# A four-layer graph network: edge payloads scattered by source inside layer 0, and one-hot matrices stored there for layer 2

## The chip, the cores and the metric

The kernel runs on one core of one Trainium2 chip. The metric is the device time of one execution in microseconds (us). It has 25,000 edges and 50,000 nodes of 64 values each.

## The reference

Four layers follow each other, each added to its input `x` after `h = relu(layernorm(x))`. All use the same edges, sorted by target (`dst`).

```python
# layer 0: messages from both ends, mean over the target's edges, update
messages = relu(concat([h[src], h[dst]]) @ W_msg + b_msg)
aggregated = segment_sum(messages, dst) / max(count(dst), 1)
x = x + relu(concat([h, aggregated]) @ W_upd + b_upd)
# layer 1: normalised sum over the edges, product
x = x + (segment_sum(h[src] * norm, dst) + h) @ W.T + b
# layer 2: attention over each target's edges (4 heads), edge-type tables,
#          two layer norms around a gelu network
x = x + layer_norm(x1 + gelu(x1 @ W1 + b1) @ W2 + b2) * g + b   # x1: after attention
# layer 3: exp(-t*L) applied to h by Taylor series over the edges, by SOURCE:
term = scale * segment_sum(edge_weight * term[dst], src) / k    # 4 x 20 terms
```

Layer 3 sums by source, while layers 0 to 2 sum by target. A Taylor term of order k is not zero only at a node from which a path of k edges leads on.

## The kernel before

**Tiling.** The function `fast` holds the work. Nodes lie in 392 blocks of 128 (`BK`); 49 groups (`NQ`) of eight blocks are the steps `q` of every layer. Each group owns 640 edge slots, five tiles of 128. So a step gathers 5 tiles of source rows with indirect DMAs on GpSimd (POOL), 128 rows each, brings edges to nodes and nodes to edges with 0/1 matrices on TensorE (PE), and stores its nodes' rows to tables in HBM.

**0/1 matrices.** `node_hot` makes `noh` (8 instructions on VectorE, DVE; from slot to node), `slot_hot` makes `soh` (5 instructions; from node to slot), by comparing keys with an iota. Layer 0 needs both, layer 1 `soh`, layer 2 both: `noh` in `hots`, `soh` in the second `message`. The keys come from `ktab`, broadcast to 128 partitions (`load_keys`).

**Preparation** (lines 1210 to 1489). Histograms of the edges (196 tiles), each edge's slot by source (`slot`, `pf`), and then the payload: `raw` holds 16 words for each edge, source, target's row, weight, and a mark whether the target has edges of its own. The mark comes from 196 gathers (`gather(raw[:, t, 3:4], otab, ...)`), and 196 scatters send the payload to its slot in the table `stab` (`scatter(stab, raw[:, t, :], pf[:, t:t + 1], ...)`). `layer0_tables` makes the norms and products of layer 0's nodes (`atab`, `btab`, `h0t`), 49 steps on DVE, ACT and PE. Between its steps the hook `region` reads each half group's edges from `fields` with a DMA on SP at an offset that a register holds (`rl`, 98 of them). From `rl` follow keys, counts (`kf`, `cnt`, `ci`, `di`), the gather rows `nrs`, and the degrees (`deg`, 49 one-hots).

**Lists for layer 3.** `build_lists` is a generator: it reads `stab` back, then `list_two` compacts the slots that have a second term (one-hots on DVE, products on PE), `flags_two` and `looks` ask with 98 gathers (`lgot`) whether the path goes on, then `list_three`, and `compact` for orders 4 to 8, each with `link`, `map_rows` and `looks` (scatters and gathers on POOL). A `Pace` runs it beside the layers: after each stage of a step it adds `rate` to its credit and takes one piece of the generator for each whole credit. The rates are 0.5 in layer 0, 0.4 in layer 1, 1.2 in layer 2. A `yield "wait"` sets the credit back.

**Layers.** `pipeline` runs the stages of a layer skewed over the steps: layer 0 has `fetch, hots, message, sums, update, project`, layer 1 `fetch, scaled, sums, turn, product`. Layer 2 has two pipelines, `up` (`fetch, hots, logits`) and `down` (`fetch2, message, sums, attend, turn, close, product, finish`), in four batches with a softmax after each batch; `down` is one batch behind. Layer 3 applies terms 1 and 2 to all nodes, and terms 3 to 8 to the lists, with `dense` for the rest.

**Order.** Each engine runs its instructions in the order that the program's scheduler wrote when the kernel was built. That order is not quite the order of the calls: an instruction is placed early when its engine is expected to be free. What it writes holds at run time. POOL runs one queue: an indirect DMA that waits holds back all behind it.

Of the kernel before, what the change touches and what calls it, by code (L numbers as in the profile page):

```python
# [55 lines left out]
BW = 3 * D  # L56
# [4 lines left out]
OHW = (0, 384, 768, 1152, 1664, 1920)  # L61

# [904 lines left out]
def fast(ctx: ExitStack, tc: tile.TileContext, a: dict, out: bass.AP, flag: bass.AP):  # L967
# [187 lines left out]
    def layer0_tables(hook):  # L1155
        with tc.tile_pool(name="pac", bufs=1) as cp, tc.tile_pool(name="pa", bufs=3) as pool, \
# [25 lines left out]
            def product(q, s):  # L1182
# [10 lines left out]
                pack(b3, bt.rearrange("p b (k d) -> p b k d", k=3))  # L1193
# [24 lines left out]
    with tc.tile_pool(name="so", bufs=1) as sp, tc.tile_pool(name="sw", bufs=4) as sw:  # L1218
# [14 lines left out]
        fld = sp.tile([P, NT, 3], I32, name="fld")  # L1233
        for i, t in enumerate((dstt, srct, typt)):
            nc.vector.tensor_copy(fld[:, :, i], t)
        nc.sync.dma_start(fields[0:EP, :].rearrange("(p t) f -> p (t f)", p=P), fld.rearrange("p t f -> p (t f)"))
# [6 lines left out]
        tail = sp.tile([P, RW * 3 // P], I32, name="tail")  # L1243
# [53 lines left out]
        nc.sync.dma_start(otab.rearrange("(p b) o -> p (b o)", p=P), hasout)  # L1297


        nrd = sp.tile([P, NT], I32, name="nrd")  # L1300
        raw = sp.tile([P, NT, PW], I32, name="raw")
        lo, hi = sp.tile([P, NT], I32, name="lo"), sp.tile([P, NT], I32, name="hi")
        nc.vector.tensor_scalar(hi, dstt, N - 1, None, op0=OP.min)
        nc.vector.tensor_scalar(lo, hi, P - 1, None, op0=OP.bitwise_and)
        nc.vector.tensor_scalar(hi, hi, 7, None, op0=OP.arith_shift_right)
        nc.vector.scalar_tensor_tensor(nrd, lo, float(BK), hi, op0=OP.mult, op1=OP.add)
# [88 lines left out]
        for t in range(NT):  # L1395
            put = scatter(stab, raw[:, t, :], pf[:, t:t + 1], P * TL - 1)
            if t:
                tc.declare_no_dep(put.ins, group="slots", reason="rows are distinct")
            tc.add_to_no_dep_group("slots", put.ins)


        rl = sp.tile([NQ, RW, 3], I32, name="rl")
# [50 lines left out]
        srci = sp.tile([P, NQ, 5], I32, name="srci")  # L1453
        with tc.tile_pool(name="ps3", bufs=3, space=PSUM) as ps:
            for row, dst in ((kf, key), (srow, srci), (ci, cinv), (di, dise)):
# [16 lines left out]
        nc.vector.tensor_copy(khi, hi)  # L1472
        deg = sp.tile([P, BK], F32, name="deg")
# [216 lines left out]
    def list_two(cols):  # L1690
# [3 lines left out]
        nc.vector.tensor_copy(live, cols[3])  # L1694
# [155 lines left out]
    def build_lists():  # L1850

        for _ in range(6):
            yield "wait"
# [27 lines left out]
    def node_hot(pool, s):  # L1881

        s.noh = pool.tile([P, 8, 2 * P], BF16, name="noh")
        for j in range(8):
            t0, n = BT[j]
            nc.vector.tensor_scalar(s.noh[:, j, :n * P], s.keys[:, t0 * P:(t0 + n) * P], pblk[:, j:j + 1], None,  # L1886
# [11 lines left out]
    def to_slots(po, s, tab, start=True):  # L1898

        for i in range(5):  # L1900
            b0, nb = TB[i]
            for j in range(b0, b0 + nb):
                c = (i - BT[j][0]) * P
                for k in range(3):
                    nc.tensor.matmul(po[:, i, :], s.noh[:, j, c:c + P], tab[:, j, k * D:k * D + D],
                                     start=(start and j == b0 and k == 0), stop=(j == b0 + nb - 1 and k == 2))
# [753 lines left out]
```

## Time and profile before

| | us |
|---|---|
| median of 13 runs | 3649.52 (3629.94 to 3668.43) |
| profiled execution, its time | 3648.63 |
| profiled execution, its span | 3646.5 |
| busy: PE, DVE, ACT, POOL | 2524.8, 2660.1, 1325.0, 2095.3 |
| mean granted TensorE clock | 0.678 |
| DMA, mean rate | 126 GB/s |

The profile is of one execution. Instruction lines give the line of the source, engine, operation, output and input by the program's names, shapes, count, then the busy time in us and the mean of one in ns, then the idle time of the engine before them and what ended most of it. "issue" is time in which the engine waited for nothing that the profile shows. A wait is attributed to the release that came last. Line numbers are those of the kernel before; the changed kernel's are higher by 2 to 16.

### The profile page before, as it was taken

Reading aid. Unit: us, or ns where it says so; the run is one execution under the profiler, and the core shown is the slowest. Engines: PE = TensorE matmul, PEld = TensorE weight load, DVE = VectorE, ACT = ScalarE, POOL = GpSimd, SP = SyncE. Lnnn points to the kernel's source line nnn. Section 1 sums busy time; section 2 is a strip of 40 time slices with the busy share of each in tenths; the row PEclk is TensorE's granted clock in tenths of the full one; section 3 lists DMA queues with packets and bytes.
Section 4 is the critical chain, followed back from the end, with each engine's and each line's share of the span. In section 5 each row is a group of like instructions: output and inputs, shape, how many; then the busy total and the mean of one; then the engine's idle time right before and its main releaser. Section 6 shows DMA issues by size and latency. Waiting matters only on the chain. (4 is left out here: it accounts for less than half of the span.)

```text
span 3646.5 us, 63671 instructions
## 1 busy us (share of the span) xinstructions
PE 2524.8 (69%) x21828; PEld 1782.3 (49%) x21828; DVE 2660.1 (73%) x8365; ACT 1325.0 (36%) x3056; POOL 2095.3 (57%) x1997
## 2 busy tenths in 40 slices
PE   7897775689999746777579667677687464456620
PEld 3324664577777634666455334344343354355520
DVE  9999988788788637999878767778888565455310
ACT  0002552222222315777405443445478333332000
POOL 0477777733334757666376775664100677674786
PEclk9755555776566857888758676778789675566555
DMA  1003772754445416787664333333222345488221
GB/s 53 6 4 108 209 228 93 188 144 123 111 126 138 121 32 182 234 241 233 183 192 141 89 106 107 99 116 99 71 89 74 117 118 155 147 234 227 44 25 11
DMA packets 528804, 457.79 MB, mean 126 GB/s; under 512 B 282147, under 2 KB 388802, under 8 KB 528340
## 3 DMA queue, kind: packets, MB, share of 16 engines
q1 hardware_dynamic: 361204, 263.52, 25.5%
q10 hardware_dynamic: 94032, 139.60, 11.1%
q0 software_dynamic: 73232, 50.49, 7.5%
q8 instruction: 174, 2.85, 0.3%
q14 instruction: 162, 1.33, 0.1%
HBM read 217.09 MB, written 237.38 MB: 125 GB/s over the span
## 5 line engine op out<-in xcount | busy, mean ns | idle before, releaser
L1006 POOL DMA_INDIRECT y<-h3tab,sptr x245 | 262.4, 1071 | 326.4 <-DVE soh L1894 252.0
L1006 POOL DMA_INDIRECT ga<-atab,nrs x245 | 248.2, 1013 | 313.2 <-DVE z L2003 144.2
L1006 POOL DMA_INDIRECT kvg<-kvtab,nrs x245 | 249.1, 1017 | 178.7 <-issue 65.5
L1006 POOL DMA_INDIRECT gt<-g1tab,nrs x245 | 254.5, 1039 | 145.6 <-issue 65.8
L1934 PEld LDWEIGHTS <-soh 128*128 128x128 bf16 x4410 | 224.1, 118 | 206.0 <-issue 192.9
L1924 PE MATMUL pa<-soh,m 128*64 128x256 bf16 (+1 forms) x2646 | 282.0, 331 | 35.8 <-ACT m L2006 24.4
L1006 POOL DMA_INDIRECT raw<-otab,nrd x196 | 194.9, 994 | 192.0 <-DVE bad L1152 132.6
L1011 POOL DMA_INDIRECT stab<-raw,pf x196 | 207.2, 1057 | 59.7 <-issue 59.4
L1924 PEld LDWEIGHTS <-m 128*64 128x64 bf16 x2646 | 178.2, 140 | 119.1 <-issue 51.0
L1934 PE MATMUL po<-y,soh 128*128 128x64 bf16 x2205 | 126.0, 232 | 133.8 <-DVE y L1086 67.4
L1006 POOL DMA_INDIRECT lgot<-nmap,ldst x183 | 183.9, 1005 | 59.8 <-issue 53.3
L1131 DVE TENSOR_REDUCE ln_v<-ln_sq 128x8 f32<-128x512 f32 x294 | 196.0, 678 | 24.8 <-ACT ln_sq L1144 18.7
L1894 DVE TENSOR_SCALAR soh<-it,key 128x384 bf16<-128x384 f16 (+2 forms) x735 | 204.7, 320 | 6.0 <-PE pa L1924 5.7
L1006 POOL DMA_INDIRECT y<-ftab,ldst x140 | 139.5, 997 | 85.4 <-issue 74.7
L1144 ACT ACTIVATE ln_sq<-ln_xc 128x512 f32<-128x512 f32 x196 | 121.0, 627 | 172.9 <-DVE ln_xc L1142 168.3
L1086 DVE TENSOR_TENSOR y<-y 128x320 f32<-128x320 f32 (+1 forms) x196 | 76.0, 391 | 146.3 <-ACT y L2493 123.0
L1886 DVE TENSOR_SCALAR noh<-keys,pblk 128x256 bf16<-128x256 f16 (+1 forms) x784 | 177.8, 288 | 2.7 <-DMA keys<-ktab 2.7
L1189 PE MATMUL pab<-wab,tr 64*128 64x128 f32 x784 | 149.8, 436 | 32.4 <-ACT tr L1176 32.4
L1132 ACT ACTIVATE ln_v<-ln_v,epsc 128x8 f32<-128x8 f32 x294 | 83.5, 296 | 228.3 <-DVE ln_v L1131 208.2
L1934 PE MATMUL po<-g,soh 128*128 128x64 bf16 x2205 | 119.6, 213 | 67.0 <-DVE g L1086 66.6
L2352 PE MATMUL ph<-tr,w1z 128*128 128x512 f32 x196 | 144.0, 825 | 27.4 <-ACT tr L2346 27.1
L1189 PEld LDWEIGHTS pab<-wab,tr 64*128 64x128 f32 x784 | 135.8, 324 | 51.4 <-ACT tr L1176 51.1
(571 smaller groups left out, 7399.3 us busy)
## 6 DMA issues: line engine op xcount, KB each, us to landing
kvtab<-kv SPq DMA_DIRECT2D x49, 512.0 KB
xs<-xstab SPq DMA_DIRECT2D x98, 256.0 KB
ftab<-f ACTq DMA_DIRECT2D x98, 256.0 KB
xt<-in_x SPq DMA_DIRECT2D x96, 256.0 KB
btab<-bt ACTq DMA_DIRECT2D x49, 384.0 KB
bt<-btab SPq DMA_DIRECT2D x49, 384.0 KB
qtab<-qt ACTq DMA_DIRECT2D x49, 384.0 KB
qt<-qtab SPq DMA_DIRECT2D x49, 384.0 KB
```

The lines of the kernel that those rows point to most:

```text
L1006: return nc.gpsimd.indirect_dma_start(out=dst, out_offset=None, in_=tab[:, :], in_offset=IndirectOffsetOnAxis(ap=idx, axis=0))
L1011: return nc.gpsimd.indirect_dma_start(out=tab[:, :], out_offset=IndirectOffsetOnAxis(ap=idx, axis=0), in_=src, in_offset=None, bounds_chec ...
L1086: nc.vector.tensor_sub(x3[:, :, k, :], x3[:, :, k - 1, :], h[:, :, k - 1, :])
L1131: nc.vector.tensor_reduce(v, sq, AX.X, OP.add)
L1132: nc.scalar.activation(v, v, AF.Sqrt, bias=epsc, scale=1.0 / D)
L1144: nc.scalar.activation(sq, xc, AF.Square)
L1189: nc.tensor.matmul(pab[:, i, :], s.tr[r, i, :], wab[r, :], start=True, stop=True)
L1886: nc.vector.tensor_scalar(s.noh[:, j, :n * P], s.keys[:, t0 * P:(t0 + n) * P], pblk[:, j:j + 1], None, op0=OP.is_equal)
L1894: nc.vector.tensor_scalar(oh[:, OHW[i]:OHW[i + 1]], it16[:, b0 * P:(b0 + n) * P], keys[:, q, i:i + 1], None, op0=OP.is_equal)
L1924: nc.tensor.matmul(o, l, r, start=first, stop=last)
L1934: nc.tensor.matmul(po[:, j, :], oh[:, c:c + P], msg[:, i, k, :], start=(not started and i == t0 and k == 0), stop=(end and (not started or ...
L2352: nc.tensor.matmul(ph, w1z[h], s.tr, start=True, stop=True)
```

## The change

The diff, cut to its core:

```diff
-BW = 3 * D
+BW = 3 * D + 2
+NOH = (0, 128, 384, 640, 896, 1152, 1408, 1664)
-    fields = dram.tile([EPD, 3], I32, name="fields")
+    fields = dram.tile([EPD, 5], I32, name="fields")
+    paytab = dram.tile([P * NQ, 5 * PW], I32, name="paytab")
-    otab = dram.tile([NN, 1], I32, name="otab")
+    ohtab = dram.tile([NQ * P, 2, OHW[-1]], BF16, name="ohtab")
...
 # layer0_tables.product
+                nc.vector.tensor_copy(bt[:, :, 0:2], hasout[:, 8 * q:8 * q + 8, None].to_broadcast([P, 8, 2]))
...
 # preparation
-        nc.sync.dma_start(otab..., hasout)
-        nc.vector.memset(raw, 0)
-        for i, f in enumerate((srct, nrd, wt.bitcast(I32))):
-            nc.vector.tensor_copy(raw[:, :, i], f)
-        for t in range(NT):
-            gather(raw[:, t, 3:4], otab, nrd[:, t:t + 1])
...
-        for t in range(NT):
-            put = scatter(stab, raw[:, t, :], pf[:, t:t + 1], P * TL - 1)
+        fld = sp.tile([P, NT, 5], I32, name="fld")          # was written first, with 3 fields
+        for i, t in enumerate((dstt, srct, typt, wt.bitcast(I32), pf)):
+            nc.vector.tensor_copy(fld[:, :, i], t)
+        nc.scalar.dma_start(fields[0:EP, :]..., fld...)
-        rl = sp.tile([NQ, RW, 3], I32, name="rl")
+        rl = sp.tile([NQ, RW, 5], I32, name="rl")
...
+        nc.vector.memset(pay, 0)                            # weight, slot, row, source by group
+        nc.scalar.dma_start(paytab..., pay...)
...
 # build_lists
-        for _ in range(6):
-            yield "wait"
+        yield "wait"
...
 # layer 0
+            nc.sync.dma_start(s.pay..., paytab...[:, q, :])          # fetch
+            nc.sync.dma_start(ohtab[P * q:P * q + P, 0, :], s.noh)   # message
+            nc.scalar.dma_start(ohtab[P * q:P * q + P, 1, :], s.soh)
-            pe = ps.tile([P, 5, D], F32, name="pe", bufs=2)
+            pe = ps.tile([P, 5, D + 2], F32, name="pe", bufs=2)
+            nc.scalar.activation(s.pay.bitcast(F32)[:, :, 3], pe[:, :, 0], AF.Copy)
+            for i in range(5):                                       # sums
+                put = scatter(stab, s.pay[:, i, :], s.pay[:, i, 4:5], P * TL - 1)
-        lists_pace.rate = 0.5
-        pipeline(range(NQ), (fetch, hots, message, sums, update, project), lists_pace)
+        pipeline(range(NQ), (fetch, hots, message, sums, update, project))
 # layer 1
-            nc.scalar.dma_start(nodes(x2tab, q), x2)
+            nc.vector.tensor_add(x2b, x2, along(b2n, 8))
+            nc.scalar.dma_start(nodes(x2tab, q), x2b)
-        lists_pace.rate = 0.4
+        lists_pace.rate = 0.8
 # layer 2
-            load_keys(pool, q, s)
+            nc.sync.dma_start(s.noh, ohtab[P * q:P * q + P, 0, :])   # fetch
-            node_hot(pool, s)                                        # hots
+            nc.sync.dma_start(s.soh, ohtab[P * q:P * q + P, 1, :])   # fetch2
-            s.soh = slot_hot(pool, key, q)                           # message
-            nc.vector.tensor_add(s.x2, s.x2, along(b2n, 8))          # finish
-            nc.vector.tensor_add(x3, x3, h)
 # layer 3
+            nc.sync.dma_start(s.h, nodes(h3tab, q))                  # fetch
+            nc.vector.tensor_add(s.xs, s.xs, s.h)                    # scaled
```

The 196 gathers of the mark and the 196 scatters by edge order go. The slot `pf` and the weight travel as two more fields to the groups; each layer 0 step scatters its five tiles, 245 in all. The mark of the target is two more columns of `btab`, and comes out of the product with `noh` in `message`. Layer 0 runs no list work; layer 1 runs it at rate 0.8. `noh` is packed to 1920 columns, and it and `soh` are stored by layer 0 to `ohtab` (480 KB each a step) and loaded by layer 2. The add of `b2n` goes from layer 2 to layer 1, and the add of `h` to layer 3.

More of the change, by code (lines that the diff above doesn't have):

```diff
@@ L1453, in fast @@
         srci = sp.tile([P, NQ, 5], I32, name="srci")
+        wrow, prow = sp.tile([NQ, RW], F32, name="wrow"), sp.tile([NQ, RW], F32, name="prow")
+        nc.vector.tensor_copy(wrow, rl[:, :, 3].bitcast(F32))
+        nc.vector.tensor_copy(prow, rl[:, :, 4])
+        nc.vector.scalar_tensor_tensor(prow, prow, -float(FAR), own, op0=OP.add, op1=OP.mult)
+        nc.vector.tensor_scalar_add(prow, prow, float(FAR))
+        pay = sp.tile([P, NQ, 5, PW], I32, name="pay")
+        nc.vector.memset(pay, 0)
         with tc.tile_pool(name="ps3", bufs=3, space=PSUM) as ps:
-            for row, dst in ((kf, key), (srow, srci), (ci, cinv), (di, dise)):
+            for row, dst in ((kf, key), (srow, srci), (ci, cinv), (di, dise), (wrow, pay[:, :, :, 2].bitcast(F32)),
+                             (prow, pay[:, :, :, 4])):
                 pt = ps.tile([P, 5, NQ], F32, name="pt")
@@ L1472, in fast @@
         nc.vector.tensor_copy(khi, hi)
+        nrow = sp.tile([P, NQ, 5], F32, name="nrow")
+        nc.vector.scalar_tensor_tensor(nrow, lo, float(BK), hi, op0=OP.mult, op1=OP.add)
+        nc.vector.scalar_tensor_tensor(pay[:, :, :, 1], rowi[:, :NQ, None].to_broadcast([P, NQ, 5]), 8.0, nrow,
+                                       op0=OP.mult, op1=OP.add)
+        nc.vector.tensor_copy(pay[:, :, :, 0], srci)
+        nc.scalar.dma_start(paytab.rearrange("(p q) f -> p (q f)", p=P), pay.rearrange("p q i f -> p (q i f)"))
         deg = sp.tile([P, BK], F32, name="deg")
@@ L1881, in node_hot @@
     def node_hot(pool, s):
-        s.noh = pool.tile([P, 8, 2 * P], BF16, name="noh")
+        s.noh = pool.tile([P, OHW[-1]], BF16, name="noh")
         for j in range(8):
             t0, n = BT[j]
-            nc.vector.tensor_scalar(s.noh[:, j, :n * P], s.keys[:, t0 * P:(t0 + n) * P], pblk[:, j:j + 1], None,
+            nc.vector.tensor_scalar(s.noh[:, NOH[j]:NOH[j] + n * P], s.keys[:, t0 * P:(t0 + n) * P], pblk[:, j:j + 1], None,
                                     op0=OP.is_equal)
@@ L1896, in slot_hot, with to_slots @@
         return oh
[L1898 removed]
+    def to_slots(po, s, tab):
         for i in range(5):
@@ L1993, in fetch @@
             load_keys(pool, q, s)
+            s.pay = pool.tile([P, 5, PW], I32, name="pay", bufs=4)
+            nc.sync.dma_start(s.pay.rearrange("p i f -> p (i f)"), paytab.rearrange("(p q) f -> p q f", p=P)[:, q, :])
         def hots(q, s):
@@ L2009, in sums @@
         def sums(q, s):
+            for i in range(5):
+                put = scatter(stab, s.pay[:, i, :], s.pay[:, i, 4:5], P * TL - 1)
+                if q or i:
+                    tc.declare_no_dep(put.ins, group="slots", reason="rows are distinct")
+                tc.add_to_no_dep_group("slots", put.ins)
             pa = ps.tile([P, 512], F32, name="pa")
@@ L2305, in fetch2 @@
             nc.sync.dma_start(s.vv.rearrange("p t d -> p (t d)"), vvtab[P * q:P * q + P, :])
+            s.soh = pool.tile([P, OHW[-1]], BF16, name="soh", bufs=3)
+            nc.sync.dma_start(s.soh, ohtab[P * q:P * q + P, 1, :])
             s.h2 = pool.tile([P, 8, D], F32, name="h2", bufs=3)
```

41 lines of the change are left out of this document (16 added, 25 removed).

## The prediction

> **What bounds the kernel now.** I read the stage view first (busy time of each engine between two times). The cuts are the first gathers of the layers, which the views by tile give: `ga` at 658.4, `gt` at 1372.6, `kvg` at 1789.3, `y<-h3tab` at 2845.4 us. The columns are stretch, length, then busy time of PE, PEld, DVE, ACT, POOL, then granted clock, DMA share, GB/s. The first four rows are preparation, layer 0, layer 1, layer 2.
>
> ```profile
> 0.00:658.00 658.00, 490.99 (x2235) 285.24 (x2235) 602.04 (x1996) 161.27 (x353) 403.39 (x398) 0.61 0.34 97
> 658.00:1372.00 714.00, 605.56 (x5901) 486.67 (x5902) 519.29 (x1836) 191.86 (x492) 343.13 (x343) 0.66 0.47 126
> 1372.00:1789.00 417.00, 301.00 (x3533) 238.11 (x3533) 371.14 (x1096) 290.20 (x882) 254.53 (x245) 0.84 0.74 221
> 1789.00:2845.00 1056.00, 747.91 (x5474) 440.34 (x5475) 828.63 (x2542) 498.10 (x825) 518.76 (x498) 0.74 0.36 108
> ```
>
> DVE bounds the preparation (602 of 658) and layer 1 (371 of 417). The 398 POOL instructions of the preparation lie beside DVE. Layer 0 and layer 2 are not one thing each, so I cut them finer: plain layer 0, layer 0 with the list work of `list_two` in it, layer 0 with the `lgot` gathers in it, and the middle of layer 2.
>
> ```profile
> 671.00:745.00 74.00, 66.95 (x816) 54.70 (x817) 62.30 (x212) 28.50 (x74) 50.19 (x51) 0.85 0.92 237
> 873.00:1040.00 167.00, 164.42 (x1374) 132.06 (x1373) 122.54 (x451) 41.45 (x108) 56.28 (x54) 0.50 0.41 114
> 1223.00:1329.00 106.00, 55.04 (x555) 44.40 (x553) 43.27 (x136) 19.63 (x50) 80.41 (x85) 0.64 0.19 54
> 2000.00:2590.00 590.00, 415.86 (x2947) 242.48 (x2946) 453.05 (x1474) 264.96 (x449) 364.84 (x346) 0.74 0.34 101
> ```
>
> By the starts of `z` a step of layer 0 takes 8.2 to 9 us plain, 16.2 us in the second row (PE full, at half clock) and 19 to 22 us in the third (POOL full). In the fourth row 346 POOL instructions stand; with 0.30 us before each they fill 365 + 104 = 469 of 590 us, and the rest is mostly POOL waiting for list values from DVE. So POOL paces the middle of layer 2.
>
> The costliest groups give the prices: count, busy us and mean ns of one, idle before it.
>
> ```profile
> L1006 POOL DMA_INDIRECT ga<-atab,nrs x245 | 248.2, 1013 | 313.2 <-DVE z L2003 144.2
> L1006 POOL DMA_INDIRECT gt<-g1tab,nrs x245 | 254.5, 1039 | 145.6 <-issue 65.8
> L1011 POOL DMA_INDIRECT stab<-raw,pf x196 | 207.2, 1057 | 59.7 <-issue 59.4
> L1894 DVE TENSOR_SCALAR soh<-it,key 128x384 bf16<-128x384 f16 (+2 forms) x735 | 204.7, 320 | 6.0 <-PE pa L1924 5.7
> L1886 DVE TENSOR_SCALAR noh<-keys,pblk 128x256 bf16<-128x256 f16 (+1 forms) x784 | 177.8, 288 | 2.7 <-DMA keys<-ktab 2.7
> ```
>
> The waits around 650 us show all that the end of the preparation owes to the scatters:
>
> ```profile
> DVE bupd_o L1104 <- DMA stab<-raw,pf: 9.4, 1, 9.4
> POOL ga L1006 <- DVE bupd_o L1109: 2.6, 1, 2.6
> ```
>
> **The change part by part**, against the profiled execution (span 3646.5, time 3648.6; the median is 3649.5). A difference below 0.3%, 11 us, cannot be told from none.
>
> **Preparation.** 196 gathers of `otab` and 196 scatters leave POOL, but they were beside DVE: only the 9.4 + 2.6 us come back. DVE gains 49 copies of `hasout` into `bt` (0.21 us, as the 128x8 rows `ln_s` have: 10 us), the zeroing of `pay` (3.3 us, from `raw`'s 2.7 us by size, which goes), and some ten small ones at 0.3 to 0.8 us: net +14. `fields` is now written only after `pf`, at some 320 us, so the 98 reads of `rl` move among the table steps on SP. They took 1.3 us each (92 in 120 us); three a step with the step's own load and store are 4.9 us of SP against a step of 5.3 us, and in the built order DVE's `kf` waits for the last read, behind the 32nd `atab` store: +6. Sum +8 (from -12, all hidden, to +40, SP late).
>
> **Layer 0 becomes POOL's.** Each step issues 5 gathers and now 5 scatters. Under DMA load a gather costs 1.04 + 0.27 us (`gt`), a scatter 1.06 + 0.30: 13.4 us a step, above the plain step's 8.2 to 9. In the built order a group of five `stab` alternates with five `ga`, four steps ahead, so POOL rarely waits for `message`. 245 of each: 320 + 333 = 653; the last 20 scatters (27) lie beside the drain; from the last `ga` to the first `gt` 47 as now; 15 until the first scatter can go. 688 against 714: -26. In exchange layer 0 loses the whole of `list_two` and its `lgot`, which is why it doesn't grow. Bounds: medians (0.94 and 0.97 us) make -77; the half-clock step of 16.2 us would make +127, but it holds list work that is gone, so I stay near POOL's price. The new stores (two of 480 KB a step) raise 1.77 MB to 2.83 MB a step; the row at 237 GB/s and 0.92 share would carry them in 11.0 us, below 13.4, so I add nothing for them. [...]
>
> **Layer 1 receives the list work.** `list_two` starts there at rate 0.8. In the built order its one-hots stand in 15 steps, `flags_two` in 7 more, then 98 `lgot` among the gathers of 9 steps. A step there takes 8.0 us now (starts of `x2`), at 1500:1760 with DVE 242 and PE 199 of 260 us busy at clock 0.86. DVE a step: (371 - 62)/49 = 6.3 without `list_three` and `link` (62 us of the 371, moved to layer 2), +0.68 for `x2b` (as L2379's 679 ns) is 7.0; `list_two` is 71 us on DVE now (L1737's one-hots 55.7), 3.3 of its 49 parts a step, 4.8. Together 11.8, at a busy share of 93% 12.7. PE: 6.1, at half clock 10.5, plus 2.9 for `list_two` (L1741's 42.9 us): 13.4 at half clock, the state of the second row above, which I take. 15 x 13.4 = 201. Flags (25 us on DVE, L1670 21.2 of it): (7.0 + 25/7)/0.93 x 7 = 80. The `lgot` stretch: 98 x 1.27 + 45 x 1.31 = 183, +4, for 14 steps. 13 plain steps at 7.5 = 98; fill and drain 25. Sum 591 against 417: +174 (from +90 if the list work costs what PE's free time leaves over, to +235). [...]
>
> **Layer 2.** Gone from DVE: 245 `soh` (66 us), 392 `noh` (87), L2379 and L2384 (33 each): 220 us. But POOL keeps 245 `kvg` and 256 list instructions. In the built order its first list scatter follows 135 `kvg`, not 115, since `list_three` now runs here: that start moves by some +64 us. From there 110 + 208 instructions before the last `kvg` (130 + 240 now, 562 us) at 1.34 us and their share of waits make 483: the last `kvg` 16 us earlier. Behind it 20 of the `finish` steps remain, 13 us each with DVE 86%, ACT 81%, PE 78% busy; without 2.6 us of DVE ACT and PE hold them at 11.5: -30. Sum -45 (from -220, all of DVE's time, to +20). The loads of the stored matrices, 960 KB a step, meet a DMA share of 0.36: hidden.
>
> **Layer 3** adds a load and 0.69 us of DVE a step where POOL's 6.5 us decide: +3.
>
> +8 - 26 + 174 - 45 + 3 = +114 on 3649.5: 3764 us.
>
> **The rivals.** (1) Layer 2 follows DVE and gives its 220 us back. For: DVE is 78% busy there, and POOL's long waits are for list values on DVE. Against: POOL is full between them. 3650 + 8 - 26 + 174 - 220 + 3 = 3589, faster; it decides once layer 2 is under 1056 - 159 = 897 us. (2) Layer 1 hides half of the list work, PE having 23% free at 1500:1760: +90 there, 3680. (3) In layer 0 the stores or the half clock bound: 16.2 us a step, +127 for -26, 3917. (4) The payloads only change place, nothing longer or shorter: 3650.
>
> **How the numbers follow.** Forecast 0.50, (1) 0.12, (2) 0.23, (3) 0.10, (4) 0.05. The range 3640 to 3870 holds the forecast with its bounds, (2) and (4); most of (1) and (3) is left out. Faster 0.12, same 0.05, slower 0.83.
>
> **What would show it.** First `ga` within 645 to 700; layer 0's steps 13 to 14 us with POOL full and no `lgot`; `gt` first at 1310 to 1400; layer 1 about 590 us with `lgot` in its last third; layer 2 about 1010 us with POOL still full in its middle. A layer 1 below 500 us, or a layer 2 below 897, makes it wrong.

## The result, and the profile after

The changed kernel takes 4044.36 us (median of 10 runs, 4031.09 to 4055.86), the kernel before 3652.05 (median of 46). The ratio is 1.107, 95% interval 1.105 to 1.110. It is slower, as forecast, but by 392 us where I forecast 114, and outside the range. The profiled execution took 4029.5 us, span 4027.7.

The runs below fell on two kinds of chip: on some, like the one of the two profiles, the kernel before takes 3648 to 3655 us, on others 4955 to 4959. Each ratio is against the kernel before on the same chip, and stages are compared only within a kind. What the traces show of the second kind is told at the end.

The stage view of the changed kernel, cut at the first `ga`, `gt`, `kvg` and `y<-h3tab` as before (820.3, 1490.4, 2138.1, 3221.4). Columns: stretch, length, busy time of PE, PEld, DVE, ACT, POOL, granted clock, DMA share, GB/s.

```profile
0.00:820.00 820.00, 491.77 (x2245) 287.28 (x2245) 614.08 (x2048) 172.91 (x353) 1.28 (x6) 0.58 0.27 79
820.00:1490.00 670.00, 531.67 (x5341) 430.35 (x5341) 433.79 (x1361) 194.66 (x539) 492.73 (x490) 0.72 0.69 211
1490.00:2138.00 648.00, 405.39 (x3820) 292.48 (x3820) 447.71 (x1345) 301.79 (x884) 357.28 (x343) 0.66 0.49 144
2138.00:3221.00 1083.00, 716.62 (x5746) 433.32 (x5746) 686.28 (x2085) 457.99 (x797) 501.59 (x498) 0.75 0.45 143
```

| | before | after | measured | forecast |
|---|---|---|---|---|
| preparation | 658 | 820 | +162 | +8 |
| layer 0 | 714 | 670 | -44 | -26 |
| layer 1 | 417 | 648 | +231 | +174 |
| layer 2 | 1056 | 1083 | +27 | -45 |
| layer 3 and end | 801 | 806 | +5 | +3 |

The preparation's DVE is busy for 614 us, 12 more than before where 14 were forecast, but the stage is 206 us longer than that. More than half of the miss is here. In layer 0 POOL has the 490 indirect DMAs; in layer 1 the clock falls from 0.84 to 0.66; in layer 2 DVE's busy time falls by 142 us net, with `list_three` and `link` (62 us in layer 1 before) added, and the stage gets no shorter.

The groups that answer to those of before (count, busy us and mean ns of one, idle before it; `soh` and `noh` in one shape each, at L1893 and L1885 where the kernel before has L1894 and L1886):

```profile
L1013 POOL DMA_INDIRECT stab<-pay x245 | 247.7, 1011 | 80.1 <-issue 69.5 <-ACT m L2012 6.3 <-ACT cat L2025 2.4
L1008 POOL DMA_INDIRECT ga<-atab,nrs x245 | 245.0, 1000 | 892.8 <-DVE bupd_w L1112 818.4 <-issue 64.9 <-DMA stab<-pay 3.7
L1893 DVE TENSOR_SCALAR soh<-it,key 128x384 bf16<-128x384 f16 x294 | 83.7, 324 | 2.5 <-PE pa L1925 2.4
L1885 DVE TENSOR_SCALAR noh<-keys,pblk 128x256 bf16<-128x256 f16 x343 | 76.6, 294 | 0.0
```

`stab` is now 245 instructions at 1011 ns, and outside the 0.28 us in the mean before each ("issue") it waits for 11 us only. `ga` waits 818 us for the whole preparation.

Where the preparation's time went is best seen in one table step. These are lines of the changed kernel's timeline, others left out; columns are start, duration, engine, line, operation, and the idle time before it with its releaser.

```profile
485.44 0.69 DVE L1147 SCALAR_TENSOR_TENSOR h<-ln_xc,ln_r 128x512 f32<-128x512 f32 x1
486.28 1.09 PE L1176 MATMUL pt<-ident,h 128*128 128x128 f32 x4 [6.68 <-DVE h L1147]
487.40 0.60 ACT L1178 ACTIVATE tr<-pt 128x512 f32<-128x512 f32 x1 [2.23 <-PE pt L1176]
488.05 3.09 PE L1191 MATMUL pab<-wab,tr 64*128 64x128 f32 x16 [0.69 <-ACT tr L1178]
490.57 0.42 DVE L1193 TENSOR_TENSOR b<-pab,b_L_gnn_b_msg 128x256 f32<-128x256 f32 x1 [4.44 <-ACT at L1192]
491.59 0.35 SPq L1197 DMA_DIRECT2D atab<-at  x1
493.39 0.68 DVE L1141 TENSOR_REDUCE ln_s<-xt 128x8 f32<-128x512 f32 x1
494.55 0.41 SPq L1063 DMA_DIRECT2D xt<-in_x  x1
```

The norm of a step (`h`), its transpose, its product and the sum `b` of the same step follow each other, and only then does DVE begin the next norm (`ln_s`). On DVE, PE and ACT hardly anything of two steps overlaps: one step takes 11.5 us, 24 times over (steps 9 to 32; the reads of `rl` end with step 32). Before, DVE began the norm of the next step before it took up the product, and a step took 5.3 us. 24 x 6.2 = 149 us. The same stretch of time before, and in the changed kernel (shown again below), has DVE busy for 45 and 22 of 50 us:

```profile
450.00:500.00 50.00, 39.40 (x195) 33.64 (x194) 44.56 (x94) 29.60 (x66) 38.59 (x38) 0.50 0.80 232
```

Steps 5 to 8 also have three reads each on SP, but their norms had been made ahead (the last at 355.6 us); `atab`'s stores of these steps go out every 5.0 us (356.9 to 376.9). Then the lead is used up: the next norm waits 10.7 us for its load of `xt`, which stands behind the reads. From there on SP waits 6.8 us in each of 20 steps (waits of SP's queue from 400 to 640 us: total, times, longest):

```profile
SPq L1197 <- ACT at L1192: 135.1, 20, 6.8
```

### The profile page after: what moved, and what is told of

Read it like the earlier page. It is cut to its first block, busy times and chain, and to the rows that moved or that the text cites. A ratio compares the mean times of both kernels' runs of the same rounds, so it can differ in the third digit from the quotient of the medians.

```text
span 4027.7 us, 63677 instructions
## 1 busy us (share of the span) xinstructions
PE 2520.2 (63%) x21838; PEld 1772.2 (44%) x21838; DVE 2546.0 (63%) x7781; ACT 1310.4 (33%) x3077; POOL 1939.0 (48%) x1850
## 5 line engine op out<-in xcount | busy, mean ns | idle before, releaser
L1008 POOL DMA_INDIRECT y<-h3tab,sptr x245 | 270.6, 1104 | 258.5 <-DVE soh L1893 184.2
L1013 POOL DMA_INDIRECT stab<-pay x245 | 247.7, 1011 | 80.1 <-issue 69.5
L1925 PE MATMUL pa<-soh,m 128*64 128x256 bf16 (+1 forms) x2646 | 257.4, 319 | 6.9 <-DVE m L1088 3.6
L2105 PE MATMUL pp<-wkv,tr 64*128 64x256 f32 x784 | 198.0, 533 | 39.8 <-ACT tr L1945 39.6
L2031 PE MATMUL po<-wupd,cat 128*128 128x64 f32 x784 | 138.1, 337 | 106.9 <-ACT cat L2025 106.8
L1925 PEld LDWEIGHTS <-m 128*64 128x64 bf16 x2646 | 166.2, 136 | 75.7 <-issue 38.8
L1176 PE MATMUL pt<-ident,h 128*128 128x128 f32 x196 | 53.9, 430 | 210.0 <-DVE h L1147 200.3
L1935 PE MATMUL po<-g,soh 128*128 128x64 bf16 x2205 | 130.0, 223 | 85.5 <-DVE g L1088 70.1
L2031 PEld LDWEIGHTS po<-wupd,cat 128*128 128x128 f32 x784 | 124.4, 244 | 123.2 <-ACT cat L2025 121.8
L1013 POOL DMA_INDIRECT nmap<-lval,lnrow x85 | 92.1, 1083 | 127.5 <-DVE lval L1639 68.2
```

Source lines behind the costliest of these rows:

```text
L1008: return nc.gpsimd.indirect_dma_start(out=dst, out_offset=None, in_=tab[:, :], in_offset=IndirectOffsetOnAxis(ap=idx, axis=0))
L1013: return nc.gpsimd.indirect_dma_start(out=tab[:, :], out_offset=IndirectOffsetOnAxis(ap=idx, axis=0), in_=src, in_offset=None, bounds_chec ...
L1176: nc.tensor.transpose(pt[:, i, :], s.h[:, 2 * i:2 * i + 2, :].rearrange("p a d -> p (a d)"), ident)
L1925: nc.tensor.matmul(o, l, r, start=first, stop=last)
L1935: nc.tensor.matmul(po[:, j, :], oh[:, c:c + P], msg[:, i, k, :], start=(not started and i == t0 and k == 0), stop=(end and (not started or ...
L2031: nc.tensor.matmul(po[:, j, :], s.cat[:, j // 4, j % 4 * P:j % 4 * P + P], wupd[j // 4], start=False, stop=(j == 7))
```

## The experiments

Stages in us by the same cuts (kernels on chips of the first kind):

| kernel | preparation | layer 0 | layer 1 | layer 2 | layer 3 | ratio to before (95%) |
|---|---|---|---|---|---|---|
| before | 658 | 714 | 417 | 1056 | 801 | 1 |
| after | 820 | 670 | 648 | 1083 | 806 | 1.107 (1.105 to 1.110) |
| b_store | 657 | 730 | 420 | 1107 | 799 | 1.014 (1.009 to 1.018) |
| b_nolist2 | 655 | 718 | 417 | 1126 | 903 | 1.049 (1.046 to 1.053) |
| a_pool_nolist2 | 656 | 668 | 649 | 984 | 1000 | 1.087 (1.082 to 1.091) |
| a_pool_nolist1 | 655 | 677 | 417 | 1257 | 829 | 1.048 (1.043 to 1.052) |
| b_lists_l2_n | 655 | 489 | 419 | 1206 | 826 | 0.988 (0.986 to 0.991) |
| b_lists_l2_r2 | 656 | 496 | 419 | 1337 | 797 | 1.013 (1.010 to 1.015) |
| b_l0slow_n | 656 | 619 | 532 | 1112 | 805 | 1.016 (1.013 to 1.019) |

On chips of the second kind:

| kernel | preparation | layer 0 | layer 1 | layer 2 | layer 3 | ratio to before (95%) |
|---|---|---|---|---|---|---|
| a_pool_reads | 655 | 999 | 801 | 1336 | 967 | 0.960 (0.957 to 0.962) |
| a_xt_pool | 764 | 1001 | 801 | 1324 | 970 | 0.981 (0.978 to 0.984) |
| b_late_fields_2 | 1260 | 934 | 584 | 1366 | 962 | 1.032 (1.027 to 1.037) |
| b_late_fields | 1280 | 936 | 586 | 1371 | 957 | 1.035 (1.033 to 1.038) |
| b_lists_l1 | 1097 | 671 | 789 | 1378 | 963 | 0.990 (0.987 to 0.992) |
| b_lists_l2 | 1097 | 694 | 588 | 1502 | 994 | 0.981 (0.978 to 0.984) |
| b_l0slow | 1096 | 767 | 711 | 1389 | 962 | 0.993 (0.991 to 0.995) |
| b_lists_l2_store | 1096 | 668 | 589 | 1461 | 989 | 0.970 (0.966 to 0.973) |
| b_l2_store_n | 1097 | 670 | 589 | 1456 | 988 | 0.969 (0.966 to 0.971) |
| b_l2_adds | 1096 | 674 | 549 | 1504 | 999 | 0.975 (0.973 to 0.978) |
| b_l2_store_adds | 1096 | 667 | 546 | 1461 | 996 | 0.963 (0.958 to 0.967) |

**The preparation: where the reads of `rl` stand.**

```diff
 # a_pool_reads (from the changed kernel; also part of the two a_pool_nolist kernels)
-  v = nc.values_load(firsti[0:1, r:r + 1], engines=(mybir.EngineType.SP,), ...)
-  moves.append(nc.sync.dma_start(rl[...], fields[...]))
+  v = nc.values_load(firsti[0:1, r:r + 1], engines=(mybir.EngineType.Pool,), ...)
+  moves.append(nc.gpsimd.dma_start(rl[...], fields[...]))
```

> The changed kernel with only the 98 reads of rl moved from SP's queue to POOL's, which has nothing to do before the first ga. Theory A: the preparation grew by 162 us because, with the reads among the table steps on SP, the written order of DVE lost its skew: from step 8 to 32 the norm of a step (h) stands directly before the product of the same step (b<-pab), so that DVE waits about 6 us in each of 25 steps of 11.5 us (5.3 us before) for transpose, copy and product. In the order of this kernel the norm is one step ahead throughout. A expects table steps of 5 to 6 us, the first ga at 660 to 700 us and a time of 3890 to 3930. Rival B: fields is written only at 320 us and the 98 reads (1.2 us each) with kf behind them are what takes the time, on whichever queue: first ga still at 780 to 830, time 4010 to 4050.

Measured: first `ga` at 654.7 us, table steps of 5.2 us. This run fell on a chip of the second kind, so its total is not the one expected; but its preparation has no indirect DMA, and up to 300 us its rows are those of the changed kernel (from 250 to 300 us DVE is busy for 46.09 us in both). The two a_pool_nolist kernels have the same edit on chips of the first kind: 655 and 656 us. The stretch 450 to 500 us of the changed kernel, and 400 to 450 us of a_pool_nolist2:

```profile
450.00:500.00 50.00, 18.19 (x86) 15.16 (x87) 22.33 (x47) 15.12 (x30) 0.00 (x0) 0.50 0.35 100
```

```profile
400.00:450.00 50.00, 39.43 (x188) 33.30 (x189) 46.30 (x106) 30.58 (x69) 17.36 (x36) 0.50 0.78 226
```

DVE does twice the work in the same time, while 36 reads go out on POOL. So fields that are written late, the extra columns and `kf` behind the last read cost nothing that can be seen when the reads are on a queue with nothing else to do; the reads on SP's queue among the table steps cost 165 us. Rival B falls.

```diff
 # a_xt_pool (from the changed kernel): the reads stay on SP, the loads of xt go to POOL
-                load_x(xt, q)
+                load_x(xt, q, nc.gpsimd)
```

> The changed kernel with the 98 reads of rl left on SP, beside atab's stores, but the loads of xt of the table steps issued by POOL. Theory A (DVE's lost skew): the norms now stand one to nine steps ahead of the products in DVE's order, so the steps fall to 5 to 7 us although SP carries the same reads and stores: first ga at 670 to 710, time 3890 to 3940. Rival C: SP itself is too slow for three reads and a store a step (11.5 us): atab's stores, which stay behind the reads, hold the at buffers and the steps remain at 11 to 12 us: first ga at 800 to 830, time about 4040.

Measured: first `ga` at 764.3; steps of 10.1 us (second kind of chip; POOL's loads here are plain DMAs, and whether these too hold up others there is not known). Neither expectation holds. In this order the norms run ahead of the products on DVE, and yet only 56 us come back. The waits of SP's queue between 400 and 640 us (us in total, times, longest) say what holds the step now:

```profile
SPq L1395 <- DMA btab<-bt: 96.4, 23, 4.9
SPq L1197 <- DMA h0t<-tr: 38.5, 24, 3.2
```

Each third read of `rl` waits 4.2 us until `btab`'s store has landed, and `atab`'s store stands behind it. So DVE's lost skew is not the whole of it: by its trace it is the link in the changed kernel, and when it is undone SP's queue, with reads that wait for landings, becomes the link. What the two have in common, the reads on SP among the steps, is the cause; that the skew alone makes the changed kernel's 165 us is read from the trace and no run shows it.

```diff
 # b_late_fields and b_late_fields_2 (from the kernel before): fields with five columns, written behind pf
-        fld = sp.tile([P, NT, 3], I32, name="fld")     # at the start, three columns
+        fld = sp.tile([P, NT, 5], I32, name="fld")     # behind pf, with wt and pf
```

> The kernel before with one part of the change alone: fields gets its five columns and is written behind pf, so that the reads of rl fall among the table steps; gathers of the mark, scatters of the payload, lists and layers are as before. In its written order DVE has lost the skew in 26 steps. Theory A: those steps take 11.5 us, first ga at 800 to 830 (658 before), and the time is 3650 + 150 = 3790 to 3820. Rival: the preparation's growth owes to the other edits (hasout's copies, pay, the extra rows of the transposes): first ga at 660 to 690, time 3650 to 3680.

> The kernel of b_late_fields, the kernel before with fields written behind pf and its 98 reads among the table steps on SP, on another chip: in the first the other engines stood still while POOL sent its 392 indirect DMAs, so that run says nothing on the reads. With the reads on POOL the changed kernel's preparation was 655 us in three runs (820 with them on SP). Theory A expects the first ga at 800 to 840 here and 3790 to 3830 in all; the rival, that another edit of the change is needed for the growth, 660 to 690 and 3650 to 3680.

Both fell on chips of the second kind, so the times expected can't be met; the first (preparation 1280 us) and the second (1260) agree within 20 us. The kernels with the preparation of before have 1096 or 1097 there: this part alone adds 164 us in the second. Its table steps, once POOL has ended at 788 us, are the 11.5 us of the changed kernel, 25 times (steps 8 to 32), and the row is the changed kernel's at twice the length:

```profile
900.00:1000.00 100.00, 34.38 (x165) 28.79 (x165) 47.45 (x90) 31.02 (x62) 0.00 (x0) 0.50 0.38 106
```

Theory A's part on the reads holds: this edit by itself makes the growth.

**Layers 0 to 2: the place of the list work.**

```diff
 # a_pool_nolist1 (from the changed kernel, reads on POOL): no list work in layer 1
-        lists_pace.rate = 0.8
-        pipeline(range(NQ), (fetch, scaled, sums, turn, product), lists_pace)
+        pipeline(range(NQ), (fetch, scaled, sums, turn, product))
```

> The changed kernel with the reads of rl on POOL and no list work in layer 1: list_two, flags_two and all that follows run in layer 2 at rate 1.2. Layer 1 (648 us in the changed kernel) falls to 420 to 460 us: that its 231 us more are the list work's. Layer 2 (1083) grows: by 150 to 230 us if the list work costs the same wherever it stands, time 3800 to 3890; by under 60 us if layer 2 has room for it (DVE 63%, POOL 46% busy), time 3680 to 3740.

Layer 1 is 417 us, as in the kernel before to the us, though `x2b` is in it: all 231 us are the list work's. Layer 2 pays 174 us more for the same work, so it has little room for it (3826 us, the first of the two cases expected).

```diff
 # b_lists_l1 (from the kernel before): the changed kernel's places of the list work
-        pipeline(range(NQ), (fetch, hots, message, sums, update, project), lists_pace)   # layer 0, rate 0.5
+        pipeline(range(NQ), (fetch, hots, message, sums, update, project))
-        lists_pace.rate = 0.4                                                            # layer 1
+        lists_pace.rate = 0.8
-        for _ in range(6):                                                               # build_lists
-            yield "wait"
+        yield "wait"
```

> The kernel before with the place of the list work changed alone: none in layer 0, rate 0.8 in layer 1, as the changed kernel has it. Payload, preparation and stored matrices are as before. If layer 1's growth by 231 us in the changed kernel is the list work's, first kvg minus first gt is 620 to 660 here (417 before). Layer 0 without lists and scatters is then bound by its plain step of 8.2 to 9.0 us: 430 to 470 us (714 before). Layer 2, where list_three now runs, 1056 to 1110. Sum: 3650 - 260 + 231 + 30 = 3650, between 3600 and 3690: what layer 0 lost is paid back in layer 1. Rival: layer 1 of the changed kernel is long for another reason (what its buffers and the new add x2b wait for), then it stays under 520 us here and the time falls below 3560.

On the second kind of chip: layer 1 is 789 us against 588 in b_lists_l2, which has none there, so 201 us for the list work by itself, without the change's other parts. Of layer 0 this run says nothing: without lists and scatters it takes 671 us here and 694 in b_lists_l2, on chips of the second kind, and 489 in b_lists_l2_n on the first.

```diff
 # b_lists_l2 and b_lists_l2_n (from the kernel before): all list work in layer 2; build_lists as in b_lists_l1
-        lists_pace.rate = 0.5
-        pipeline(range(NQ), (fetch, hots, message, sums, update, project), lists_pace)
+        pipeline(range(NQ), (fetch, hots, message, sums, update, project))
-        lists_pace.rate = 0.4
-        pipeline(range(NQ), (fetch, scaled, sums, turn, product), lists_pace)
+        pipeline(range(NQ), (fetch, scaled, sums, turn, product))
 # b_lists_l2_r2: also rate 2.0 for 1.2 in layer 2; b_l0slow: only rate 0.25 for 0.5 in layer 0
```

> The kernel before with the whole list work in layer 2 (none in layers 0 and 1, rate 1.2 in layer 2); payload and scatters stay in the preparation, matrices are not stored. In the changed kernel list_two and flags_two cost 231 us in layer 1, and 174 us when put in layer 2 (1257 for 1083). What layer 0 gives back for them is open, since in the changed kernel POOL's scatters hold it at 670. My reading: without lists and scatters its steps are the 8.2 to 9.0 us of its plain stretch, 440 to 490 us in all (714 before); layer 1 417; layer 2 1056 + 174 = 1200 to 1270: 3540 to 3620, faster than before. Rival G: layer 0 without lists runs into the half clock of its long stretch, 13 to 16 us a step: 640 to 720, time 3740 to 3850.

> The kernel of b_lists_l2 (the kernel before with the whole list work in layer 2) on another chip, since in its first run POOL's indirect DMAs held up the other engines in every stage. As there: if the plain step of 8.2 to 9.0 us carries through a layer 0 without lists and scatters, layer 0 takes 440 to 490 us (714 before), layer 2 1200 to 1280, time 3540 to 3640, faster than before; with 13 us steps or more, 640 to 720 and 3740 to 3850. In the first case layer 0 of the changed kernel (670) is 200 us of POOL's scatters; in the second its scatters cost nothing over what PE takes anyhow.

> As b_lists_l2_n, with rate 2.0 for 1.2 in layer 2, so that in POOL's order all lists end before layer 2's last kvg and none stands among layer 3's gathers. Layer 0 as there; layer 2 1180 to 1300, layer 3 800 to 815 where the other has 820 to 900. Between 40 us faster and 30 us slower than b_lists_l2_n.

b_lists_l2_n takes 3611.09 us, 0.988 of the kernel before (interval 0.986 to 0.991), and is the one version on the first kind of chip that is faster than the kernel before, by little; on the second kind it has 0.981. Layer 0 without lists and scatters takes 489 us, 9.0 us in most steps (440 to 490 expected, 640 to 720 by rival G). Its middle, and below it the middle of layer 0 in the changed kernel:

```profile
700.00:1100.00 400.00, 373.29 (x4668) 305.82 (x4667) 363.48 (x1157) 166.88 (x429) 217.03 (x211) 0.92 0.67 190
```

```profile
850.00:1430.00 580.00, 468.22 (x4720) 378.53 (x4718) 376.28 (x1166) 172.24 (x480) 444.99 (x444) 0.74 0.71 214
```

The same work of PE and DVE needs 400 us in the one and 580 in the other. In the second, POOL has 444 instructions, 445 us, with 0.30 us before each 578 of 580: it is full. No gap between its indirect DMAs from 900 to 1420 us is above 1 us. The changed kernel and the two a_pool_nolist kernels have that layer 0 in 668 to 677 us, so payload and stores cost it 179 to 188 us.

r2 moves the list work out of layer 3 (797 us), as expected, and loses 131 us in layer 2: 3703.18, 92 us behind, where 30 was the most expected. More list work at a time was dearer there.

> The kernel before with one number changed: the rate of the list work in layer 0 is 0.25 for 0.5, so that list_two stretches over the whole of layer 0 and its 98 lgot fall into layer 1. If list work costs its place whatever the density, layer 0 loses the 106 us of its lgot stretch less what 45 plain steps need there (60 us) and layer 1 gains 80 to 130 us: time 3640 to 3720. If the thin list work stays beside the plain steps at full clock, layer 0 falls to 560 to 620 us and the time to 3540 to 3620.

> The kernel of b_l0slow (rate 0.25 for 0.5 in layer 0) on another chip. If list work costs its place whatever its density: layer 0 620 to 660, layer 1 500 to 550, time 3640 to 3720. If thin list work stays beside the plain steps: layer 0 560 to 620, time 3540 to 3620.

Thin list work is not cheaper: layer 0 falls to 619, where the two cases meet, layer 1 grows to 532, as in the first case; layer 2 grows by 56, which neither case had, and the time is 3714.66. In layer 0, and over what layers 1 and 2 take in the kernel before, the lists cost 130 + 115 + 56 = 301 us here, and 225 in the kernel before (714 - 489). On the second kind of chip it is 4924.6, 0.993 (0.991 to 0.995).

**Layer 2: the stored matrices.**

```diff
 # b_store (from the kernel before): node_hot packed to 1920 columns, as in the change, and
+            nc.sync.dma_start(ohtab[P * q:P * q + P, 0, :], s.noh)       # layer 0, message
+            nc.scalar.dma_start(ohtab[P * q:P * q + P, 1, :], s.soh)
-            node_hot(pool, s)                                            # layer 2
-            s.soh = slot_hot(pool, key, q)
+            nc.sync.dma_start(s.noh, ohtab[P * q:P * q + P, 0, :])
+            nc.sync.dma_start(s.soh, ohtab[P * q:P * q + P, 1, :])
```

> The kernel before with the matrices' part alone: noh packed to 1920 columns, noh and soh stored by layer 0 (two stores of 480 KB a step) and loaded by layer 2, where 392 noh and 245 soh instructions go from DVE (153 us). Payload, preparation and place of the list work as before. My reading: layer 2 is ordered by POOL's queue, in which the list work's dependent gathers and scatters stand between the kvg, so it keeps 1000 to 1060 us (1056 before), and layer 0, with a DMA share of 0.41 to 0.47, takes the stores for 0 to 40 us (714 before): 3620 to 3690 in all. Rival D: layer 2 follows DVE: 850 to 930 us, time 3450 to 3530. Rival E: the stores slow layer 0's POOL gathers and PE's stretch: layer 0 over 780, time over 3720.

Layer 0 takes the stores for 16 us (DMA share 0.64). Layer 2 is 51 us longer with 128 us less of DVE. All three cases missed it. In the written order the list work moved forward: all 42 scatters of `nmap` for `list_three` stand among the first 85 `kvg`, where the kernel before sends 115 `kvg` first; the 106th `kvg` goes out 226 us into the layer, before at 148. DVE's free time was given to list work, and POOL's queue made the layer wait for it. This is read from the order and the trace; an order with the matrices and the old start of the lists was not tried. How a wait passes on in that queue the kernel before shows: one `kvg` waits 25.2 us for DVE's `vv`, until 2220.7 us, and four more `kvg` and then the `nmap` follow it, each 0.30 us behind the last.

```diff
 # b_nolist2 (from the kernel before) and a_pool_nolist2 (from the changed kernel, reads on POOL)
-        lists_pace.rate = 1.2
+        lists_pace.rate = 0.0
```

> The kernel before with no list work in layer 2: list_three and what follows run in layer 3 instead. Layer 2 is then 245 kvg on POOL (320 us) and about 740 us of DVE: if DVE decides there, 780 to 830 us (1056 before). Layer 3 grows by what the lists take, 150 to 350 us. If layer 2 stays above 950 without the lists, POOL's list work isn't what paces it.

> The changed kernel with the reads of rl on POOL (first ga at 655) and no list work in layer 2. Without the lists the matrices' saving on DVE can show: DVE has about 600 us of work left in layer 2, and the layer takes 640 to 720 us, 80 to 170 less than layer 2 of the kernel before without its lists. That is my reading: the saving of 220 us of DVE was real, and lay beside POOL's list chains. Rival F: PE, ACT or the loads of the matrices pace layer 2, so that it takes as long as in the kernel before without lists, within 30 us. Layer 1 keeps its 650 us with the list work in it.

The stage times mislead here: `list_three` and what follows were still written ahead of layer 3's first gather, so they lengthen layer 2's end. I cut at the last product with `kvg` (`kk`) instead. The part of layer 2 up to there, with the list work and without: before and b_nolist2, after and a_pool_nolist2.

```profile
1789.00:2564.00 775.00, 555.36 (x4543) 342.39 (x4543) 596.39 (x2033) 312.85 (x549) 512.09 (x493) 0.72 0.41 119
```

```profile
1789.00:2476.00 687.00, 538.71 (x4472) 333.07 (x4472) 551.26 (x1673) 297.45 (x532) 252.80 (x245) 0.75 0.46 133
```

```profile
2138.00:2929.00 791.00, 520.42 (x4753) 329.95 (x4753) 483.80 (x1610) 288.98 (x529) 470.77 (x470) 0.73 0.50 158
```

```profile
1972.00:2478.00 506.00, 427.44 (x4276) 278.47 (x4278) 372.85 (x1013) 223.88 (x434) 245.02 (x245) 0.77 0.70 226
```

Without list work this part takes 687 us in the kernel before, and 506 with the stored matrices: 181 us less, the size of the DVE work that left it (178 us less busy). `kvg` then waits for DVE's `vv`, in b_nolist2 and a_pool_nolist2 (the same two stretches):

```profile
POOL kvg L1006 <- DVE vv L2249: 316.8, 30, 21.4
```

```profile
POOL kvg L1008 <- DVE vv L2263: 149.1, 25, 32.5
```

With the lists the part is 775 and 791, and these waits are 37 and 72 us. The lists' share of it is 259 and 226 us of POOL, and 45 and 111 us of DVE (`list_three` is in the second). So the saving is real and is lost to the list work. The edit takes away the lists' POOL and DVE work together; that POOL's queue is the place where it is lost is read from the waits and from POOL's larger share, and is not shown by itself. My reading holds in kind. In size it missed: the whole layers, 1126 and 984, are not the 780 to 830 and 640 to 720 expected, since the lists returned in the tail.

**Parts on the second kind of chip.**

```diff
 # b_lists_l2_store = b_l2_store_n: b_lists_l2 with b_store's edits
 # b_l2_adds: b_lists_l2 with the change's x2b in layer 1 and s.xs + s.h in layer 3
 # b_l2_store_adds: both
```

> As b_lists_l2, and layer 0 stores the matrices and layer 2 loads them. Layer 0 then has two stores of 480 KB a step more at steps of 8 to 9 us, 2.8 MB a step: at the 237 to 248 GB/s that the densest stretches of the trace reached this is 11.4 us a step, so layer 0 takes 540 to 600 us; layer 2 gains up to the 150 us of DVE: 1060 to 1250. Time 3520 to 3660. If it lies above b_lists_l2 by over 30 us, the stored matrices lose more in layer 0 than they give in layer 2.

> b_lists_l2 (all list work in layer 2, scatters in the preparation, 489 us in layer 0 with steps of 9.0 us) with the matrices stored by layer 0 and loaded by layer 2; its first run fell on a chip where POOL's indirect DMAs held up the other engines. At the 237 to 248 GB/s of the densest stretches 2.8 MB a step take 11.4 us for 9.0: layer 0 560 to 610, layer 2 between 1060 and 1210 (1206 without): 3560 to 3690. If the two stores cost nothing in layer 0 (under 510), it is faster than b_lists_l2's 3611.

> b_lists_l2 with the third part of the change alone: b2n added in layer 1, h added in layer 3. Layer 1 keeps 417 to 425 (49 adds of 0.68 us beside POOL and ACT), layer 3 gains 0 to 5 us, layer 2 loses 66 us of DVE: 0 to 40 us less. 3570 to 3620.

> The change without its payload part (scatters and mark stay in the preparation), with all list work in layer 2: stored matrices and moved adds. With a_pool_nolist1 (the same, but with the payload's scatters in layer 0, and 3826 us) it prices the scatters' new place: layer 0 there 677, here 489 to 610, so 70 to 190 us. Layer 2 1200 to 1260 as there. 3580 to 3760.

All four ran on chips of the second kind, where every stage is longer (b_lists_l2: 1097, 694, 588, 1502 and 994 us, b_lists_l2_n 655, 489, 419, 1206 and 826), so what was expected is not tested. The stores give 41 to 47 us in layer 2 and cost layer 0 nothing there (667 to 670 us, without them 674 and 694); the adds alone leave layer 2 as it is (1504 for 1502), and layer 1, which has one add a step more, takes 549 for 588; why is not known. Both together come to 0.963; b_l2_store_n, on another chip of that kind, gives 0.969 (0.966 to 0.971) where b_lists_l2_store gave 0.970. The lowest two there, not told apart, are b_l2_store_adds and a_pool_reads (0.960), in which 392 indirect DMAs leave the preparation. On the first kind a_pool_reads was not run; the changed kernel's time less the 165 us of the preparation would be some 3880 there, an estimate, and slower than before: the order of versions need not be the same. How far the scatters and how far the stores make layer 0's 179 to 188 us stays without a run of its own on the first kind; that POOL is full, and that the stores cost 16 us in b_store, speaks for the scatters.

## Why the prediction was wrong, point by point

**Preparation, the step that failed: +8 forecast, +162 measured.** The prediction said that "the 98 reads of `rl` move among the table steps on SP", priced "4.9 us of SP against a step of 5.3 us", took +6 for `kf` and set the upper bound at +40. SP's own time was right: of an 11.5 us step it waits 6.8, so its work is 4.7, and steps 5 to 8 went at 5.0. What the sum left out, as far as the trace tells it, is that a queue with those reads in it changes the order in which everything else is written: the loads of `xt` came behind them, DVE's norm and product of a step ended up side by side, and the 4.4 us in which DVE waits for transpose, copy and product, with the shorter waits inside the norm, were paid in each of 24 steps. The written order of DVE showed it before the run; I had read it for `kf` alone. a_pool_reads, the a_pool_nolist kernels and b_late_fields_2 show the reads on SP as the cause; a_xt_pool shows that a restored lead alone gives back 56 us of it, since reads on SP then wait for `btab`'s stores, a wait that the sum did not have either.

**Layer 0: -26 forecast, -44 measured; right.** POOL sets the step: 13.1 us for 13.4, ten instructions at 1.00 to 1.01 us and 0.30 us before each. (The lower bound of -77 is about -70 by the prices it names.) But the bargain was worse than I wrote: layer 0 without lists and payload takes 489 us, the lists cost it 225, the payload and stores 179 to 188. In the preparation those scatters were beside DVE for nothing: it is 655 to 656 us with them (b_nolist2) and without (a_pool_nolist1).

**Layer 1: +174 forecast, +231 measured; the cause right, the limit not shown.** That the list work makes the growth is shown by a_pool_nolist1. The stretch of `list_two` and `flags_two`, and that of the `lgot`:

```profile
1580.00:1845.00 265.00, 211.53 (x1811) 143.27 (x1811) 211.50 (x722) 123.55 (x354) 106.05 (x100) 0.62 0.48 142
1845.00:2031.00 186.00, 67.70 (x691) 52.38 (x689) 77.99 (x195) 63.14 (x190) 142.42 (x144) 0.63 0.37 107
```

20 steps at 13.3 us (the forecast had 15 at 13.4 and 7 at 11.4, 281 us; measured 265), then 186 us for the `lgot` (187 forecast). The 13.4 was PE full at half clock. The row does not show that: PE and DVE are each busy for 212 of 265 us, the clock is 0.62, and POOL waits 127 us for ACT's `g`. That the steps came out at 13.3 is in part luck, and what paces them no run separates. Two terms were mis-sized. The `lgot` stretch holds 45 `gt`, nine steps and not "14 steps": 20 steps remain for 13, 144 us with the fill for 98. And the drain behind the last `gt` took 53 us, where I had 25 (it is 48 in the kernel before).

**Layer 2: -45 forecast, +27 measured.** Rival (1) is out: DVE's time did not come back. The reason given, POOL's queue, fits the waits. The size does not: the list work starts 84 us later (64 forecast) and from there the last `kvg` takes 493 us (483), so that it goes out 741 us into the layer, 16 us later than before (725) and not 16 earlier; and the end behind it takes 342 us, 11 more and not 30 less. It carries 45 POOL instructions of the late lists for 16 before; the forecast's own counts (256 in all, 208 ahead of the last `kvg`) put them there, and it gave them no price. What paces that end now no run separates.

**The rivals.** None came true. (2), half of layer 1 hidden, went the other way. (3) came nearest in number (3917 for 4044), by the wrong stage: layer 0's steps took 13.1 us in the mean, not 16.2.

The forecast of layer 1 took the half clock from the list stretch of layer 0 before (PE 164 of 167 us, clock 0.50). In layer 0 that clock came with the lists: in b_lists_l2_n, without them, PE is busy 373 of 400 us at 0.92. In layer 1's list stretch the clock was 0.62, and no run here shows what lowers it.

## What to carry to other kernels

Work that hides beside another engine costs nothing where it is and its full price where its own engine sets the pace: 392 indirect DMAs were free in the preparation on the first kind of chip (655 to 656 us with them and without), and 245 scatters, with stores whose share is not separated, made a 9.0 us step 13.1 in layer 0. When instructions enter a queue between the steps of a pipeline, read the written order of every engine for the lead of one stage over the next, since the occupation of the queue doesn't show a lost overlap. Time taken off an engine comes back only if that engine is what the queue in front of it waits for, and the freed time may pull other work into that queue (layer 2 of b_store: 128 us less DVE, 51 us more time).

## What the runs showed of the hardware that was not expected

In the preparation on the chips of the second kind the other engines stand still for most of the time while POOL sends its indirect DMAs. (They are three, each used in one set of runs; whether the chip or something else of that set makes it is not known.) The rows are 250 to 300 us of the kernel before (first kind), b_lists_l1 and a_pool_reads (second kind), in the same loop of DVE and PE:

```profile
250.00:300.00 50.00, 46.48 (x115) 14.30 (x114) 47.43 (x172) 0.00 (x0) 37.83 (x40) 0.50 0.02 2
```

```profile
250.00:300.00 50.00, 10.53 (x22) 2.19 (x21) 8.61 (x29) 0.00 (x0) 37.73 (x40) 0.50 0.02 1
```

```profile
250.00:300.00 50.00, 46.49 (x116) 14.48 (x115) 46.09 (x174) 0.00 (x0) 0.00 (x0) 0.50 0.00 1
```

With 40 indirect DMAs on POOL, DVE gets through 172 instructions on the first kind and 29 on the second; on the second without them 174. The instructions that ran took their usual time (`junk` of this loop 0.62 us behind gaps of 2.9 and 7.1 us in b_lists_l1, at 402 and 410 us, and 0.62 in the kernel before), and the gaps before them are mostly put down to "issue" and "remote", releases whose origin the profile does not show, and not to data, as in the waits of b_lists_l1 from 150 to 350 us:

```profile
PEld L1371 <- issue: 117.7, 40, 10.1
DVE junk L1375 <- remote: 67.4, 15, 9.9
```

The preparation takes 1097 us there for 658, and 655 without the 392 indirect DMAs (a_pool_reads); the kernel before takes 4955 to 4959 us for 3648 to 3655. What starves there was not found.
